# Who makes which half of an attention tile: GpSimd on first halves only, VectorE on both

## The chip, the core and the metric

The kernel runs on one core of a Trainium2 chip. The core has a matrix engine (TensorE, PE in the profile), a vector engine (VectorE, DVE), an activation engine (ScalarE, ACT), a general engine (GpSimd, POOL) and a queue engine for transfers (SyncE, SP). Each takes its instructions in its own order and waits for others through semaphores. The metric is the time of one execution on the device, in microseconds.

## What is computed

The input is `x` of 64 x 256 x 128 (64 graphs, 256 nodes, 128 features) and one 256 x 256 adjacency matrix. Four layers follow one another; each starts with a layer norm and a relu, and adds its result to `x`. Layer 0 is a gated unit of five steps, layer 1 a Chebyshev convolution, layer 2 a graph convolution with a norm. The last one matters here:

```python
s1 = jnp.einsum('bkf,ef->bke', x, W1)
s2 = jnp.einsum('bkf,ef->bke', x, W2)
pre = s1[:, :, None, :] + s2[:, None, :, :] + b_lin
h = jnp.where(pre >= 0, pre, ALPHA * pre)
e = jnp.einsum('bije,e->bij', h, a) + bias
attn = jax.nn.softmax(e, axis=2)
out = jax.nn.sigmoid(jnp.einsum('bij,bjf->bif', attn, x))
```

Here `W`, the weight matrix of the layer, is the adjacency matrix itself, so `e` runs over 256 features. For each of the 64 graphs, `pre` has 256 x 256 x 256 elements: a nonlinear function of every pair of nodes and every feature, which must be made element by element and then summed over the features with weights `a`.

## The kernel before

**Pairs and slots.** Graphs are taken two at a time: 32 pairs (`NPAIR`). The weights are folded in beforehand, and features are sorted by the sign of their weight, so that what is left of the nonlinear part is a maximum of s1 and -s2 (up to terms that are added elsewhere), times +1 or -1. The 256 features are two halves of 128, one feature to a partition. The first half is called a, the second b. For each pair there are 64 slots (`SLOTS`); a slot stands for a set of rows i of the attention matrix, and each of its two halves is one tile of 128 x 2048 elements: four groups of rows, two graphs, 256 nodes. In all there are 2048 slots (`NSLOT`), so 4096 half tiles. Seventeen tile buffers (`rl`, `TILES`) are shared by all of them.

**Who can make a half.** Each engine has its own form (`work_on_tile`, line 969):

- VectorE makes a whole tile in one instruction, a minimum of the broadcast `s1` and of the product `s2`, which it reads from the PSUM bank that TensorE wrote (line 988).
- ScalarE makes it in eight instructions, relu of `s1 - s2`, with `s1` as the bias and `s2` from its PSUM bank (line 996).
- GpSimd makes it in eight instructions, a minimum with a scalar, from copies of `s2` in SBUF, since it doesn't read PSUM here (line 1002). The copies are made by ScalarE: `s2c` for the first half (line 769) and `s2n` for the second (line 808).

`part_of` (line 925) says which kind an engine takes next. There are three kinds: 0 is a first half, 1 is a second half that is scored by itself, 2 is a second half that is summed onto its first half before both are scored as one tile. Before the change VectorE always takes kind 0, ScalarE always kind 1, and GpSimd takes kind 2 whenever that is not more than two slots ahead of the others (`AHEAD_OF`), and otherwise whichever of 0 and 1 lags.

**Summed slots.** For one third of the slots (`JOINED`, 650 of them, none among the last 96) the two halves are added by a DMA that accumulates, mostly two slots to a transfer (`add_pair`, line 1036). GpSimd issues it. TensorE then scores the sum once and not the halves twice.

**Scoring.** `score` (line 1090) multiplies a tile with a window of weights into a PSUM bank that collects the scores of 32 rows x 4 groups; `win` is for tiles of ScalarE and `win_n` for the others, with the opposite sign. Then `tail` makes the softmax and the output.

**The front.** `front` (line 512) computes layers 0 to 2 of a pair and the operands of layer 3, while the slots of the pair before are worked on. Its end touches the change: product `s2a` into a bank (765), copy `s2c` (769), product `s2b` into another bank (804), copy `s2n` (808), `s1b` (816) and `s1a` (825). The banks stay taken until the last half that reads them is made: `left` counts these, and `work_on_tile` gives a bank back to `spare` (line 1012).

**What sets the order.** The program is written out by a planner in the kernel's own Python (from line 1165). It keeps a clock for each engine, with an assumed duration for every kind of step (2.2 us for a VectorE tile, 1.46 us for four relus of ScalarE, 0.873 us for two instructions of GpSimd), takes the engine whose clock is least, and lets it do what is ready: steps of a tail first, then of a front (held back so that it doesn't run ahead), then half tiles; for TensorE scores come last. `in_order` ties the instructions of each engine to this order. The framework below adds semaphore waits between engines for every dependence that it sees, on tiles and on PSUM banks; the planner doesn't see these waits, only its own readiness times.

Of the kernel before, what the change touches and what calls it, by code (L numbers as in the profile page):

```python
# [10 lines left out]
OP = mybir.AluOpType  # L11
# [11 lines left out]
PE, DVE, ACT, POOL = ENGINES = (mybir.EngineType.PE, mybir.EngineType.DVE, mybir.EngineType.Activation, mybir.EngineType.Pool)  # L23
SLOTS = 64
SHARE = (1, 3)
AHEAD_OF = 2
ALONE = 96
LOW = 1
TILES = 17
# [4 lines left out]
def kernel(  # L34
# [50 lines left out]
    nc = tc.nc  # L85
    B, N, D = x.shape
# [34 lines left out]
    def ran(engine, us, *after):  # L121
        start = max(clock[engine], 0.0, *after)
        clock[engine] = start + us
        return clock[engine] + SEEN[engine]
# [6 lines left out]
    spare = [[b, 0.0] for b in banks]  # L131
# [26 lines left out]
    last, done = {}, [0]  # L158
# [325 lines left out]
    PROJECT, MIX, TURN, PRODUCT, PRODUCTS = (None, 0.44, 0.86), (None, 0.88, 1.74), (None, 0.48, 0.70), (None, 0.45, 0.88), (None, 1.33, 2.64)  # L484
    COPY, BIASED, TANH, ELEMENTS = (None, 0.34, 0.50), (None, 0.40, 0.59), (None, 0.41, 0.59), (None, 0.36, 0.61)
# [23 lines left out]
    READY = {}  # L509
    OF_FIRST = {}  # L510

    def front(p, batches):
# [4 lines left out]
        nb = len(batches)  # L517
# [18 lines left out]
        def kept(name, shape, **kw):  # L536

            if not alone:
                return work.tile([P, NB, *shape], F32, name=name, **kw)
            if name not in OF_FIRST:  # L540
                OF_FIRST[name] = work.tile([P, NB, *shape], F32, name=name, **kw)
            return OF_FIRST[name][:, own]

        def seen(b):
            return by_feature(b[0], nb)
# [14 lines left out]
        t = yield from norm(x0, 20.0 if p else 3.0, h)  # L560
        yield PE, t, 1
        b = take()
        to_feature(b[0], h)
        t_h = t
        t = ran(PE, TURN[nb], t, b[1])
        yield ACT, t
        hT, t_hT = copied("hT", b, t)
        for step in range(STEPS):
            yield PE, t_h, 1, lambda: "adj" in SET_UP
            b = take()  # L570
            mix_nodes(b[0], h, adj_t)
            t = ran(PE, MIX[nb], t_h, b[1])
            yield ACT, t
            mT, t_m = copied("h", b, t)
            if alone:
# [6 lines left out]
                t = ran(PE, PROJECT[nb], t_m)  # L582
# [5 lines left out]
                r = take()  # L588
            else:
# [4 lines left out]
                t = ran(PE, 2 * PROJECT[nb], t_m, t_hT, pr[1])  # L594
                yield ACT, t, 1
                r = take()
            nc.scalar.activation(seen(r), seen(pr), AF.Tanh, bias=br, scale=0.5)  # L597
            t = ran(ACT, TANH[nb], t, r[1])
# [5 lines left out]
            if alone:  # L604
# [5 lines left out]
                t = ran(PE, PROJECT[nb], t_rh)  # L610
            else:
# [6 lines left out]
                t = ran(PE, 2 * PROJECT[nb], t_rh, pv[1])  # L618
# [6 lines left out]
            if alone:  # L625
                nc.scalar.activation(seen(pv), seen(pv), AF.Tanh, bias=bh, scale=1.0)
                t = ran(ACT, TANH[nb], t)
                yield DVE, t
                nc.vector.tensor_sub(d, seen(pv), hT)
                t = ran(DVE, ELEMENTS[nb], t)  # L630
                spare.append([pv[0], t])
            else:
                nc.scalar.activation(seen(pv), seen(pv), AF.Tanh, bias=bh_n, scale=-1.0)  # L633
                t = ran(ACT, TANH[nb], t)
                yield DVE, t
                nc.vector.tensor_add(d, seen(pv), hT)  # L636
                t = ran(DVE, ELEMENTS[nb], t)
# [3 lines left out]
            t = ran(DVE, ELEMENTS[nb], t, t_z)  # L641
# [4 lines left out]
            t_hT = ran(DVE, ELEMENTS[nb])  # L646
            spare.append([pr[0], t_hT])
            yield PE, t_hT, 1
            b = take()
            to_token(b[0], hT)  # L650
            t = ran(PE, TURN[nb], t_hT, b[1])
# [9 lines left out]
        t = ran(DVE, ELEMENTS[nb], t)  # L661
# [6 lines left out]
        b = take()  # L668
        mix_nodes(b[0], h, adj_n)
        t = ran(PE, MIX[nb], t_h, b[1])  # L670
# [3 lines left out]
        b = take()  # L674
        to_feature(b[0], h)
        t = ran(PE, TURN[nb], t_h, b[1])
        yield ACT, t
        hT, t = copied("hT", b, t)
# [6 lines left out]
        b = take()  # L685
        mix_nodes(b[0], h, adj_2)
        t = ran(PE, MIX[nb], t_h, b[1])
        yield ACT, t
        c2T, t = copied("h", b, t)
# [5 lines left out]
        t = ran(PE, PRODUCTS[nb], t, t_po)  # L695
        yield DVE, t
        if alone:
            pt = rows_of(turned_of(po))
            nc.vector.tensor_add(pt, pt, bias1.unsqueeze(1).to_broadcast([P, nb * NC, D]))
            t = ran(DVE, ELEMENTS[nb], t)  # L700
# [3 lines left out]
        t = ran(DVE, ELEMENTS[nb])  # L704
# [4 lines left out]
        t = yield from norm(x2, t, h)  # L709
# [7 lines left out]
        b = take()  # L717
        mix_nodes(b[0], h, adj_ti)
        t = ran(PE, MIX[nb], t, b[1])
        yield ACT, t  # L720
        yT, t = copied("h", b, t)
# [5 lines left out]
        t = ran(PE, PRODUCT[nb], t, t_po)  # L727
        if alone:
# [3 lines left out]
            t = ran(DVE, ELEMENTS[nb], t)  # L732
# [3 lines left out]
        t = ran(ACT, COPY[nb], t)  # L736
# [3 lines left out]
        t = ran(DVE, ELEMENTS[nb], t)  # L740
        yield POOL, t
        inverse_root(rn, rn, MOST_POSITIVE, OP.min, NORM_EPS * NORM_EPS, OP.max)
        t = ran(POOL, 1.45, t)

        yield DVE, t, 0, lambda: p < 2 or (p - 2, NC - 1) in TAILED
        x3 = kept("x3", [NC, D])
# [3 lines left out]
        t = ran(DVE, LAST[nb], t)  # L750
# [3 lines left out]
        h3 = kept("h3", [NC, D + 1])  # L754
        nc.gpsimd.memset(h3[:, :, :, D:D + 1], 2.0)
        t = yield from norm(x3, t, h3)
        yield PE, t, 1
        b = take()
        to_feature(b[0], h3)
        t = ran(PE, TURN[nb], t, b[1])  # L760
        yield ACT, t
        hT, t_hT = copied("hT", b, t)
        yield PE, t_hT, 1
        s2a = take()
# [3 lines left out]
        s2c = kept("s2c", [N])  # L768
# [3 lines left out]
        b = take()  # L772
# [4 lines left out]
        t = ran(PE, 0.25, t_hT, b[1])  # L777
# [4 lines left out]
        t = ran(ACT, 0.2, t)  # L782
# [6 lines left out]
        s1o = kept("s1o", [NC])  # L789
# [3 lines left out]
        for k in range(2):  # L793
            nc.sync.dma_start(row[k, 0:nb * N].rearrange("(q g i) -> g q i", g=4, i=32),
                              quarter[k:P:32, 0:cols].rearrange("g (q i) -> g q i", i=32))
            t = moved(t) if k else max(t, moved(t) - 2.2)
        rows = kept("rows", [2, N])[:, 0] if alone else work.tile([P, 2, NB, N], F32, name="rows")
        nc.sync.dma_start(rows if alone else rows.rearrange("p k b n -> p k (b n)"), row[:, 0:nb * N].unsqueeze(0).to_broadcast([P, 2, nb * N]))
        lin, s2o = (rows[:, k].unsqueeze(1) if alone else rows[:, k] for k in range(2))
        t = moved(t) + 1.5  # L800
        t_lin = t
        yield PE, t_hT, 1
        s2b = take()
        project(s2b[0], w2n[:, P:2 * P], hT)
        t = ran(PE, PROJECT[nb], t_hT, s2b[1])
        yield ACT, t
        s2n = kept("s2n", [N])
        nc.scalar.copy(s2n, seen(s2b))
        t_2 = ran(ACT, COPY[nb], t)
        yield PE, t_hT, 1  # L810
        b = take()
        project(b[0], w1[:, P:2 * P], hT)
        t = ran(PE, PROJECT[nb], t_hT, b[1])
        yield ACT, t
        s1b = kept("s1b", [N])
# [4 lines left out]
        b = take()  # L820
        project(b[0], w1[:, 0:P], hT)
        t = ran(PE, PROJECT[nb], t_hT, b[1])
        yield ACT, t
        s1a = kept("s1a", [N])
        nc.scalar.activation(s1a, seen(b), AF.Identity, bias=blin_s[:, 0:1], scale=1.0)
        t_n = ran(ACT, BIASED[nb], t)
        spare.append([b[0], t_n])
        ops = dict(x3=x3, h3=h3, s1=(s1a, s1b), s2a=seen(s2a), s2b=seen(s2b), bank=[s2a, s2b], s2c=s2c, s2n=s2n, s1o=s1o, s2o=s2o,
                   lin=lin, t_lin=t_lin, since=(max(t_n, t_s2a), max(t_b, t_2), max(t_b, t_2)), alone=alone,
                   left=[0, 0])  # L830
        for u in batches:
            READY[p, u] = ops
            for n in range(p * SLOTS + u * SLOTS // 2, p * SLOTS + (u + 1) * SLOTS // 2):
                ops["left"][0] += 1
                ops["left"][1] += n not in WITH
        tiles.extend([t, max(t_b, t_n, t_lin)] for t, _ in lent)

    def across(u):
# [66 lines left out]
    begun = {}  # L905
    made = []
    left = {}
# [3 lines left out]
    WITH = set(JOINED)  # L911
# [6 lines left out]
    def where(n):  # L918
        return (n // SLOTS, n % SLOTS // 32), n % 32

    def slot(k):

        return ORDER[k][following[k]] if following[k] < len(ORDER[k]) else NSLOT

    def part_of(e):

        if e == DVE:
            return 0
        if e == ACT:
            return 1  # L930
        if slot(2) <= max(slot(0), slot(1)) + AHEAD_OF:
            return 2
        return 0 if slot(0) < slot(1) else 1

    def tile_ready(e):

# [9 lines left out]
    def row_of(u, s1, r):  # L946

        i = s1.rearrange("p b (c g i) -> p g c b i", c=NC, g=4)
        return i[:, :, :, 0, r:r + 1] if READY[u]["alone"] else i[:, :, u[1], :, r:r + 1]
# [19 lines left out]
    def work_on_tile(e):  # L969
        if e not in begun:  # L970
            k = part_of(e)
            begun[e] = [slot(k), k, *chosen(slot(k), k), 0]
            following[k] += 1
            held[e] += 1
            if k < 2:
                READY[where(begun[e][0])[0]]["left"][k] -= 1
        n, k, t, free, part = begun[e]
        u, r = where(n)
        ops = READY[u]
        rows = row_of(u, ops["s1"][min(k, 1)], r)  # L980
        since = max(ops["since"][k], free)

        def other(s2, b):
            return s2[:, 0 if ops["alone"] else b, :]

        if e == DVE:
            whole = [P, 4, NB, N]
            nc.vector.tensor_tensor(t, rows.to_broadcast(whole), ops["s2a"].unsqueeze(1).to_broadcast(whole), op=OP.min)  # L988
            done = ran(DVE, 2.2, since)
            ops["bank"][0][1] = max(ops["bank"][0][1], done)  # L990
            parts = 1
        elif e == ACT:
            parts = 2
            for g in (2 * part, 2 * part + 1):
                for b in range(NB):
                    nc.scalar.activation(t[:, g, b, :], other(ops["s2b"], b), AF.Relu, bias=rows[:, g, b], scale=-1.0)  # L996
            done = ran(ACT, 1.46, since)
            ops["bank"][1][1] = max(ops["bank"][1][1], done)
        else:
            parts = 4  # L1000
            for b in range(NB):
                nc.gpsimd.tensor_scalar(t[:, part, b, :], other(ops["s2n" if k else "s2c"], b), rows[:, part, b],  # L1002
                                        MOST_NEGATIVE, op0=OP.min, op1=OP.max)
            done = ran(POOL, 0.873, since)
        begun[e][4] += 1
        if part + 1 == parts:
            del begun[e]
            if n in WITH:
                pairs.setdefault(n, {})[k] = done, t, e
            else:  # L1010
                made.append((done, n, k, t, e))
        if k < 2 and not ops["left"][k] and ops["bank"][k] and not any(b[1] == k and where(b[0])[0] == u for b in begun.values()):
            spare.append(ops["bank"][k])
            ops["bank"][k] = None

    def pair_ready():

# [220 lines left out]
```

## Time and profile before

| what | value |
|---|---|
| median of 3 runs | 4700.0 us (4699.17 to 4700.02) |
| the profiled execution | 4698.46 us |
| its span, first to last instruction | 4696.7 us |
| granted TensorE clock, mean | 0.999 |
| DMA queue of the additions (POOL's) | 80.2% of 16 engines |

The page gives for each engine its busy time, its share of the span and its number of instructions; a chain of waits, which is followed back from the last instruction; and groups of instructions by line and shape, with busy time, mean duration and the idle time of the engine just before them. Instructions of one engine overlap each other, so the mean duration of one is longer than the time that one more of them adds (busy time divided by number, or the pitch in a timeline).

In steady state all four engines work through: between 2000 and 3000 us PE is busy 997.13 us, DVE 993.53, ACT 990.51 and POOL 988.76.

### The profile page before, as it was taken

How to read it: one execution, taken by the hardware profiler on the slowest of the kernel's cores; microseconds unless marked ns; L12 is line 12 of the kernel's file. 1: busy time of each engine (PE TensorE's matmuls, PEld its weight loads, DVE VectorE, ACT ScalarE, POOL GpSimd, SP SyncE). 2: the span in 40 equal slices, each digit the busy share in tenths (PEclk: the TensorE clock that was granted, in tenths of full speed). 3: DMA queues.
4: the chain of work that ended last, by engine and by line, in shares of the span. 5: the costliest groups of instructions: out<-in, count | busy, mean ns of one | idle time of the engine just before them, and what ended most of it. 6: DMA issues, size and time to landing. Idle time of an engine off the chain costs nothing.

```text
span 4696.7 us, 131312 instructions
## 1 busy us (share of the span) xinstructions
PE 4665.0 (99%) x51191; PEld 1765.1 (38%) x51191; DVE 4602.0 (98%) x3646; ACT 4590.1 (98%) x11987; POOL 4540.5 (97%) x9757
## 2 busy tenths in 40 slices
PE   9999999999999999999999999999999999999999
PEld 4433333433333433433333343333333333333333
DVE  5999999999999999999999999999999999999998
ACT  5999999999999999999999999999999999999999
POOL 2999999999999999999999999999999999999998
PEclk9999999999999999999999999999999999999999
DMA  1888998889988898988988989889888898898840
GB/s 28 168 159 164 167 168 161 162 159 168 167 164 165 155 167 162 170 167 156 166 166 162 168 161 168 163 166 168 160 160 167 163 169 165 161 162 165 159 78 4
DMA packets 133930, 725.02 MB, mean 154 GB/s; under 512 B 10936, under 2 KB 46136, under 8 KB 50104
## 3 DMA queue, kind: packets, MB, share of 16 engines
q0 software_dynamic: 88800, 681.60, 80.2%
q1 hardware_dynamic: 43784, 35.01, 2.5%
q8 instruction: 400, 6.55, 0.5%
q14 instruction: 226, 1.85, 0.1%
q10 hardware_dynamic: 720, 0.00, 0.0%
HBM read 26.48 MB, written 8.52 MB: 7 GB/s over the span
## 4 chain that ended last, share of the span: by engine, by line
PE 83%; DVE 7%; ACT 4%; POOL 4%; DMA 1%; issue 1%; POOLq 0%; DVEq 0%; ACTq 0%
PE bank L1106 53%; PE bank L428 26%; DVE rl L988 6%; POOL rl L1002 3%; ACT rl L996 3%; PE bank L461 2%; DMA rl<-rl 1%; PE bank L453 1%; ACT h L506 0%; POOL mv L423 0%; POOL rl L1053 0%; DVE r L636 0%; DVE bank L640 0%; DVE hT L644 0%; PE bank L776 0%
## 5 line engine op out<-in xcount | busy, mean ns | idle before, releaser
L988 DVE TENSOR_TENSOR rl<-s1a,bank 128x2048 f32<-128x2048 f32 x1757 | 3925.4, 2275 | 7.1 <-PE bank L1106 3.6
L996 ACT ACTIVATE rl<-bank,s1b 128x256 f32<-128x256 f32 x9808 | 3886.1, 710 | 0.9 <-PE bank L1106 0.3
L1002 POOL TENSOR_SCALAR rl<-s2n,s1b 128x256 f32<-128x256 f32 x6576 | 3054.4, 698 | 18.7 <-ACT s1b L816 7.5
L1106 PE MATMUL bank<-rl,win_n 128*32 128x512 f32 x17760 | 2250.5, 593 | 8.0 <-DVE rl L988 4.6
L1106 PE MATMUL bank<-rl,win 128*32 128x512 f32 x9808 | 1321.4, 593 | 0.0
L1002 POOL TENSOR_SCALAR rl<-s2c,s1a 128x256 f32<-128x256 f32 x2328 | 1083.2, 616 | 3.1
L1106 PEld LDWEIGHTS bank<-rl,win_n 128*32 128x32 f32 x17760 | 601.3, 110 | 1156.4 <-issue 959.7
L1106 PEld LDWEIGHTS bank<-rl,win 128*32 128x32 f32 x9808 | 336.6, 110 | 630.2 <-issue 508.8
L428 PE MATMUL bank<-h,wts 128*32 128x512 f32 x3720 | 467.1, 592 | 0.8 <-ACT bank L597 0.8
L1053 POOL DMA_DIRECT2D rl<-rl x350 | 406.9, 1174 | 4.3 <-POOL rl L1002 3.3
L428 PE MATMUL bank<-adj_t,h 128*32 128x256 f32 x4960 | 302.0, 381 | 2.3 <-ACT h L655 1.9
L428 PEld LDWEIGHTS bank<-h,wts 128*32 128x32 f32 x3720 | 126.1, 110 | 265.3 <-issue 209.1
L428 PEld LDWEIGHTS bank<-adj_t,h 128*32 128x32 f32 x4960 | 164.1, 110 | 160.6 <-issue 48.5
L553 ACT COPY h<-bank 128x512 f32<-128x512 f32 x217 | 166.3, 780 | 16.2 <-PE bank L428 14.9
L506 ACT ACTIVATE h<-xin,mv 128x128 f32<-128x128 f32 x372 | 166.2, 631 | 16.0 <-POOL mv L502 15.4
L428 PE MATMUL bank<-hT,wts 128*32 128x512 f32 x1240 | 167.0, 593 | 0.0
L428 PE MATMUL bank<-r,u5t 128*32 128x512 f32 x1240 | 166.8, 592 | 0.0
L597 ACT ACTIVATE bank<-bank,gate_b 128x512 f32<-128x512 f32 (+1 forms) x165 | 136.0, 824 | 17.1 <-PE bank L428 12.8
L423 POOL TENSOR_TENSOR mv<-mv,minus_half 128x4 f32<-128x4 f32 (+1 forms) x132 | 133.7, 1013 | 11.0
L620 ACT ACTIVATE bank<-bank,gate_b 128x512 f32<-128x512 f32 (+1 forms) x165 | 133.7, 810 | 9.3 <-PE bank L428 9.1
L633 ACT ACTIVATE bank<-bank,gate_b 128x512 f32<-128x512 f32 x155 | 129.0, 832 | 2.9 <-PE bank L428 2.9
L636 DVE TENSOR_TENSOR r<-bank,hT 128x512 f32<-128x512 f32 x155 | 105.6, 681 | 14.9 <-ACT bank L633 14.6
(204 smaller groups left out, 2983.0 us busy)
## 6 DMA issues: line engine op xcount, KB each, us to landing
rl<-rl POOLq DMA_DIRECT2D x300, 2048.0 KB, 14.7
rl<-rl POOLq DMA_DIRECT2D x50, 1024.0 KB, 12.1
rows<-row SPq DMA_DIRECT2D x31, 512.0 KB
xin<-in_x_dram SPq DMA_DIRECT2D x64, 128.0 KB
out_dram<-o SPq DMA_DIRECT2D x63, 128.0 KB
row<-r SPq DMA_DIRECT2D x62, 2.0 KB
rows<-row SPq DMA_DIRECT2D x2, 256.0 KB
rl<-in_L_gnn_w_w_dram SPq DMA_DIRECT2D x3, 128.0 KB
```

Source lines behind the costliest of these rows:

```text
L423: nc.gpsimd.tensor_tensor(t, t, minus_half[:, 0:t.shape[1]], op=OP.pow)
L428: nc.tensor.matmul(o[g:g + 32], w[:, g:g + 32], t, start=start, stop=stop, skip_group_check=True)
L506: nc.scalar.activation(h[:, k, :], s[:, k, :], AF.Relu, bias=mv[:, k, 0:1], scale=mv[:, k, 1:2])
L553: nc.scalar.copy(c, seen(bank))
L597: nc.scalar.activation(seen(r), seen(pr), AF.Tanh, bias=br, scale=0.5)
L620: nc.scalar.activation(seen(pr), seen(pr), AF.Tanh, bias=bz, scale=0.5)
L633: nc.scalar.activation(seen(pv), seen(pv), AF.Tanh, bias=bh_n, scale=-1.0)
L988: nc.vector.tensor_tensor(t, rows.to_broadcast(whole), ops["s2a"].unsqueeze(1).to_broadcast(whole), op=OP.min)
L996: nc.scalar.activation(t[:, g, b, :], other(ops["s2b"], b), AF.Relu, bias=rows[:, g, b], scale=-1.0)
L1002: nc.gpsimd.tensor_scalar(t[:, part, b, :], other(ops["s2n" if k else "s2c"], b), rows[:, part, b], MOST_NEGATIVE, op0=OP.min, op1=OP.max)
L1053: nc.gpsimd.dma_start(out=into, in_=of, accum_op=OP.add, max_dma_last_dim=8192)
L1106: nc.tensor.matmul(pe[g * 32:(g + 1) * 32, :], w[:, 31 - r:63 - r], flat(t[:, g]), start=False, stop=(left[u] == 0), skip_group_check=True)
```

## The change

GpSimd makes first halves only. VectorE makes every second half that is summed (kind 2) and otherwise first or second halves, whichever lags; ScalarE goes on making second halves that are scored alone. VectorE reads the second operand where ScalarE reads it, in the PSUM bank of `s2b`. So the copy `s2n` is dropped, and the count that gives back the bank of `s2b` now includes the summed second halves.

```diff
+LEAD = 0
...
         s2b = take()
         project(s2b[0], w2n[:, P:2 * P], hT)
-        t = ran(PE, PROJECT[nb], t_hT, s2b[1])
-        yield ACT, t
-        s2n = kept("s2n", [N])
-        nc.scalar.copy(s2n, seen(s2b))
-        t_2 = ran(ACT, COPY[nb], t)
+        t_2 = ran(PE, PROJECT[nb], t_hT, s2b[1])
...
-                ops["left"][1] += n not in WITH
+                ops["left"][1] += 1
...
     def part_of(e):
 
-        if e == DVE:
+        if e == POOL:
             return 0
         if e == ACT:
             return 1
         if slot(2) <= max(slot(0), slot(1)) + AHEAD_OF:
             return 2
-        return 0 if slot(0) < slot(1) else 1
+        return 0 if slot(0) <= slot(1) + LEAD else 1
...
-            if k < 2:
-                READY[where(begun[e][0])[0]]["left"][k] -= 1
+            READY[where(begun[e][0])[0]]["left"][min(k, 1)] -= 1
...
-            nc.vector.tensor_tensor(t, rows.to_broadcast(whole), ops["s2a"].unsqueeze(1).to_broadcast(whole), op=OP.min)
+            nc.vector.tensor_tensor(t, rows.to_broadcast(whole), (ops["s2b"] if half else ops["s2a"]).unsqueeze(1).to_broadcast(whole), op=OP.min)
             done = ran(DVE, 2.2, since)
-            ops["bank"][0][1] = max(ops["bank"][0][1], done)
+            ops["bank"][half][1] = max(ops["bank"][half][1], done)
...
-                nc.gpsimd.tensor_scalar(t[:, part, b, :], other(ops["s2n" if k else "s2c"], b), rows[:, part, b],
+                nc.gpsimd.tensor_scalar(t[:, part, b, :], other(ops["s2c"], b), rows[:, part, b],
                                         MOST_NEGATIVE, op0=OP.min, op1=OP.max)
...
-        if k < 2 and not ops["left"][k] and ops["bank"][k] and not any(b[1] == k and where(b[0])[0] == u for b in begun.values()):
-            spare.append(ops["bank"][k])
-            ops["bank"][k] = None
+        if not ops["left"][half] and ops["bank"][half] and not any(min(b[1], 1) == half and where(b[0])[0] == u for b in begun.values()):
+            spare.append(ops["bank"][half])
+            ops["bank"][half] = None
```

Every line after 27 has another number in the changed kernel: the tile instructions are at 985 (VectorE), 993 (ScalarE) and 999 (GpSimd) there, the scores at 1103.

## The prediction

> **What bounds the kernel now.** I read the page's first part, then its chain of waits.
>
> ```profile
> span 4696.7 us, 131312 instructions
> PE 4665.0 (99%) x51191; PEld 1765.1 (38%) x51191; DVE 4602.0 (98%) x3646; ACT 4590.1 (98%) x11987; POOL 4540.5 (97%) x9757
> ```
>
> ```profile
> PE 83%; DVE 7%; ACT 4%; POOL 4%; DMA 1%; issue 1%; POOLq 0%; DVEq 0%; ACTq 0%
> ```
>
> All four compute engines are full; TensorE ends the chain by a nose (83% of it). An edit that only moves work between DVE, ACT and POOL can therefore gain little: PE's own 4665.0 us remain. But every engine has only 30 to 155 us of idle time, so a new wait on any of them shows in the span at once. Next the costliest groups, which are the halves that the change redistributes.
>
> ```profile
> L988 DVE TENSOR_TENSOR rl<-s1a,bank 128x2048 f32<-128x2048 f32 x1757 | 3925.4, 2275 | 7.1 <-PE bank L1106 3.6
> L996 ACT ACTIVATE rl<-bank,s1b 128x256 f32<-128x256 f32 x9808 | 3886.1, 710 | 0.9 <-PE bank L1106 0.3
> L1002 POOL TENSOR_SCALAR rl<-s2n,s1b 128x256 f32<-128x256 f32 x6576 | 3054.4, 698 | 18.7 <-ACT s1b L816 7.5
> ...
> L1002 POOL TENSOR_SCALAR rl<-s2c,s1a 128x256 f32<-128x256 f32 x2328 | 1083.2, 616 | 3.1
> ```
>
> The names after the arrow matter. DVE reads s1a and a PSUM bank (the product s2a); ACT reads s1b and another PSUM bank (s2b); POOL reads only copies in SBUF, of which s2n is the one that goes away. So today the bank of s2b has one steady reader, ACT, and the bank of s2a has one, DVE. The idle column says that neither ever waits for the other: 0.9 us before ACT's 9808 instructions, 7.1 us before DVE's 1757.
>
> **The change by parts.** The copy that goes is this group (all instructions of ACT by form):
>
> ```profile
> L808 ACT COPY s2n<-bank 128x512 f32<-128x512 f32 x31 | 22.4, 721 | 0.2
> ...
> L808 ACT COPY s2n<-bank 128x256 f32<-128x256 f32 x2 | 0.8, 379 | 0.0
> ```
>
> 33 copies, 23.2 us counted with overlap. ACT's instructions overlap each other, so I price by pitch, from the timeline near the end, where both engines run one kind alone:
>
> ```profile
> 4658.45 24.26 DVE L988 TENSOR_TENSOR rl<-s1a,bank 128x2048 f32<-128x2048 f32 x11
> 4659.25 28.24 ACT L996 ACTIVATE rl<-bank,s1b 128x256 f32<-128x256 f32 x76
> ```
>
> (Start, duration, what.) A DVE tile takes (24.26 - 2.275) / 10 = 2.20 us. An ACT relu takes (28.24 - 0.67) / 75 = 0.368 us, 0.67 being its median duration. ACT's other 2179 instructions then take (4590.1 - 9808 x 0.368) / 2179 = 0.45 us each. The copies are thus worth 33 x 0.45 = 15 us of ACT. That is the whole gain that the change offers, and as PE is the bound, little of it could reach the end.
>
> POOL's halves cost the same from either operand: 3054.4 / 6576 = 0.464 us and 1083.2 / 2328 = 0.465 us. In the built program the amounts hardly move: DVE 1751 tiles (932 first halves, 819 second) for 1757, ACT 9832 relus for 9808, POOL 8928 instructions for 8904, 347 additions by DMA (303 double, 44 single) for 350; PE's instructions are the same in number. So: DVE -6 x 2.2 = -13 us, ACT +24 x 0.368 = +9, POOL +24 x 0.464 = +11; all lie beside PE's work. GpSimd's queue holds 3 issues fewer (1.17 us each), and SP's transfers are the same.
>
> **What it adds.** DVE's 819 second halves read the same PSUM bank that ACT's relus read. The waits in the built program say what becomes of that: 770 of the 819 DVE tiles carry a wait for the last ACT relu on that bank, and 793 ACT relus carry a wait for a DVE second-half tile on that bank. In the program of before no relu waits for a DVE tile that reads its bank (122 wait for a DVE first half, for other reasons). Both engines run their queues in order, so the bank is used in turns: ACT finishes its group, DVE makes its tile while ACT's next relu stands in the queue, then ACT goes on. The kernel's planner knows nothing of this: it wrote the order as if both ran at once.
>
> By operand, the order has 773 places where DVE's second-half tiles (783 of them; 10 places have two) stand between two ACT groups of one pair; the other 36 stand at a pair's ends, where ACT is already or still on another bank, and block nothing. I call the 773 places stops and sum ACT's time line over the span:
>
> - ACT's work: 4590.1 - 15 + 9 = 4584 us.
> - DVE's tiles in the stops, ACT standing still: 783 x 2.20 = 1723 us.
> - The hand-over, twice per stop. The nearest rows (timelines of the start and of the end):
>
> ```profile
> 45.03 0.45 ACT L597 ACTIVATE bank<-bank,gate_b 128x256 f32<-128x256 f32 x1 [1.75 <-PE bank L428]
> 45.51 0.42 DVE L601 SCALAR_TENSOR_TENSOR rl<-bank,rl 128x256 f32<-128x256 f32 x1 [0.74 <-ACT bank L597]
> ...
> 4690.02 0.08 DVE L856 DVE_READ_ACCUMULATOR2_ANT nmx<- 128x1 f32 x1
> ...
> 4690.14 0.91 ACT L863 ACTIVATE sc<-sc,nmx 128x256 f32<-128x256 f32 x2 [2.66 <-DVE nmx L856]
> ```
>
>   45.51 - 45.48 = 0.03 us from ACT to DVE, 4690.14 - 4690.10 = 0.04 back. Besides, an engine that must drain pays its last instruction in full and not by pitch: DVE 2.275 - 2.20 = 0.075, ACT at least 0.45 (the shortest relu) - 0.368 = 0.08, at most 0.710 (the mean) - 0.368 = 0.34. That makes 0.23 to 0.49 us per stop. I take 0.25, near the lower end, since a group that starts after a pause runs as the short rows do: 773 x 0.25 = 193 us.
> - What hides: ACT's instructions that read other things and stand in its queue within a stop. 758 stops have a wait on both sides; 314 of these have none in between, 245 one, 97 two, the rest more. At 0.45 us each and at most a stop's length, that is 396 us.
> - Stops at which DVE comes later than ACT. Between two stops ACT has 5.5 us of work on the average (4153 / 758) and DVE 3.9 (2919 / 758); pricing each gap by both, DVE is the later in 54, by 57 us together.
> - ACT's idle time of before stays: 4696.7 - 4590.1 = 107 us, of which 51 lie in the first 150 us.
> - New waits for PE, POOL and the additions, since the planned order no longer fits: no row shows them. Bounds: nothing, and three times the 107 us, 321. I take 56, the idle time outside the start once more, as PE, POOL and DMA all get slack.
>
> Sum: 4584 + 1723 + 193 - 396 + 57 + 107 + 56 = 6324 us of span. The profiled execution has 1.8 us around its span (4698.46 - 4696.7), and the median of the runs shown is 1.5 above it: 6324 + 3 = 6327, say 6330 us, or +35%.
>
> Behind ACT's blocked relu stand the front's copies and tanh (PE waits for them), behind DVE's blocked tile its gate products; each of these moves with the two engines. PE needs 4665 us of 6330, POOL about 4550: neither takes over. DMA's 80% on the additions' queue thins to 60%.
>
> The Trainium skill speaks against the change, in PSUM — Partial Sum Buffer, section "PSUM bank collisions raise a hardware error": two engines on one bank and partition quadrant at once are an error, reads against reads included, so software has to keep them apart. No row of before shows two such readers. By that rule the waits can't be spared, and the sum is the one above; were such reads free, it would be 4690.
>
> PE will now pause often, so its clock counts. The granted clock was 0.95 from 80 to 100 us, where PE was busy 16.75 of 20 us, and 0.68 in the last 7 us, where it was busy 2.0. It would decide only if it fell below 4665 / 6330 = 0.74 on the average. TensorE: Matmul & The Clock Gate, "Part 1: The HAM clock gate", says that the clock halves after an idle window of about 3.4 us. At half clock throughout PE's work would be 9330 us by that page; pauses as long as a stop (2.5 us) are shorter than its window.
>
> **Rivals.**
> 1. The bank alone. All of ACT's other work slips into the stops or into gaps: 9832 x 0.368 + 1723 + 193 + 57 + 107 = 5698 us. For it: ACT's other work (980 us) is shorter than the stops. Against it: ACT's queue is in order, and 314 of 758 stops have nothing to slip in. Anything up to 6100 I count here: 0.09.
> 2. Turn-taking spreads. A DVE tile that waits for its buffer, which PE frees late, holds ACT as well. Price: another 0.7 us per stop, 773 x 0.7 = 541, so 6870 us. For it: 606 of the 819 DVE tiles also wait for PE. Against: PE idles a quarter of the time. 0.11.
> 3. No slower: the stops fall where ACT pauses anyway, and the 15 us of copies decide. Price: 4700 - 15 = 4685 at best. It decides only if a stop costs ACT under 15 / 773 = 0.02 us, against 2.20 + 0.25 = 2.45 as worked out, and ACT has 107 us of pauses to hide 1723. 0.01; that the change doesn't do what it says is excluded by the built program, where the copies are gone and the tiles are moved. 0.01 for that the bound is elsewhere in an unseen way and time stays equal.
>
> The forecast has 0.78. A measurement of this kernel tells 0.2% (9 us) from no change: faster 0.01, same 0.01, slower 0.98.
>
> **The range.** Downwards, hand-over at 0.23 (-15), no DVE lateness (-57), relus at the pitch of eight in mid-kernel, 2.84 / 8 = 0.355 (9832 x 0.013 = -128): 6130, and some of rival 1: 6090. Upwards, hand-over at 0.49 (+185) and waits at half their bound (+105) give 6620, and part of rival 2: 6700.
>
> **What would show it.** ACT's idle time before L993 (L996 of before) grows from 0.9 us to well over 1200 us, nearly all released by DVE's L985; DVE's before L985 grows too, released by ACT's L993. Busy shares fall to about 73% on all four engines, the chain alternates DVE and ACT, PE's share of it collapses. DVE's tile stays at 2275 ns, with s1b as with s1a. I am wrong if ACT's idle time is named after PE or DMA, if the granted clock is under 0.9, or if DVE and ACT records on one bank overlap.

## The result, and the profile after

The changed kernel takes 6191.44 us (median of 6 runs, 6189.27 to 6193.57) against 4700.1 us before: a ratio of 1.3172, with a 95% interval of 1.3155 to 1.3189. It was forecast at 6330 us. The first lines of its page:

```profile
span 6190.9 us, 131780 instructions
PE 5305.7 (86%) x51191; PEld 1870.1 (30%) x51191; DVE 4660.6 (75%) x3640; ACT 4652.3 (75%) x11978; POOL 4589.2 (74%) x9778
```

The work is the same: ACT, DVE and POOL are busy for 49 to 62 us more than before, in a span that is 1494 us longer. All three stand still a quarter of the time. The groups say where (the last columns are the idle time of the engine just before the group, and what ended most of it):

```profile
L993 ACT ACTIVATE rl<-bank,s1b 128x256 f32<-128x256 f32 x9832 | 3792.6, 533 | 1459.6 <-DVE rl L985 1350.2
L999 POOL TENSOR_SCALAR rl<-s2c,s1a 128x256 f32<-128x256 f32 x8928 | 4060.4, 588 | 387.3 <-PE bank L1103 335.8
L985 DVE TENSOR_TENSOR rl<-s1b,bank 128x2048 f32<-128x2048 f32 x819 | 1871.8, 2287 | 1367.2 <-ACT rl L993 1319.6
...
L985 DVE TENSOR_TENSOR rl<-s1a,bank 128x2048 f32<-128x2048 f32 x932 | 2102.8, 2279 | 0.7 <-PE bank L1103 0.4
```

ACT's relus waited 0.9 us in all before the change and wait 1459.6 now. DVE's first halves, whose bank nobody else reads all the time, wait 0.7 us; its second halves wait 1367.2, ended by ACT's relus. Neither engine's instruction got longer: the DVE tile takes 2279 ns with s1a and 2287 with s1b. The list of who waited for whom gives the numbers of waits (sum in us, times, longest):

```profile
ACT rl L993 <- DVE rl L985: 1350.2, 692, 3.6
DVE rl L985 <- ACT rl L993: 1319.6, 699, 4.8
```

The other 109 us of the 1459.6 are named after PE, POOL and the like, but they are turns too: of the 752 pauses of ACT before a relu, 751 end within 0.2 us after a second half of DVE on the same bank (the records of the trace, put beside the operands in the built program).

And the timeline of ACT and DVE shows two such turns (start, duration; in brackets the idle time before):

```profile
3011.75 1.59 ACT L993 ACTIVATE rl<-bank,s1b 128x256 f32<-128x256 f32 x4
3013.37 2.29 DVE L985 TENSOR_TENSOR rl<-s1b,bank 128x2048 f32<-128x2048 f32 x1 [3.02 <-ACT rl L993]
3015.69 1.57 ACT L993 ACTIVATE rl<-bank,s1b 128x256 f32<-128x256 f32 x4 [2.35 <-DVE rl L985]
```

ACT ends four relus at 3013.34, DVE starts 0.03 us later, ends at 3015.66, ACT starts 0.03 us later, and so on. Nowhere in this stretch do the two run together on the bank, and in the whole trace no record of the 819 second halves overlaps a relu on the same bank. DVE waited 3.02 us for its turn, and ACT then 2.35 us for its own.

The chain of waits no longer helps: it is followed back over 15% of the span only, and there it alternates between ACT (7%) and DVE (4%).

### The profile page after: what moved, and what is told of

The parts are those of the page before. It is cut to its first block, busy times and chain, and to the rows that moved or that the text cites. A ratio compares the mean times of both kernels' runs of the same rounds, so it can differ in the third digit from the quotient of the medians.

```text
span 6190.9 us, 131780 instructions
## 1 busy us (share of the span) xinstructions
PE 5305.7 (86%) x51191; PEld 1870.1 (30%) x51191; DVE 4660.6 (75%) x3640; ACT 4652.3 (75%) x11978; POOL 4589.2 (74%) x9778
## 5 line engine op out<-in xcount | busy, mean ns | idle before, releaser
L993 ACT ACTIVATE rl<-bank,s1b 128x256 f32<-128x256 f32 x9832 | 3792.6, 533 | 1459.6 <-DVE rl L985 1350.2
L999 POOL TENSOR_SCALAR rl<-s2c,s1a 128x256 f32<-128x256 f32 x8928 | 4060.4, 588 | 387.3 <-PE bank L1103 335.8
L985 DVE TENSOR_TENSOR rl<-s1b,bank 128x2048 f32<-128x2048 f32 x819 | 1871.8, 2287 | 1367.2 <-ACT rl L993 1319.6
L1103 PE MATMUL bank<-rl,win_n 128*32 128x512 f32 x17736 | 2388.4, 608 | 47.3 <-DVE rl L985 46.6
L985 DVE TENSOR_TENSOR rl<-s1a,bank 128x2048 f32<-128x2048 f32 x932 | 2102.8, 2279 | 0.7 <-PE bank L1103 0.4
L1103 PE MATMUL bank<-rl,win 128*32 128x512 f32 x9832 | 1711.1, 613 | 84.4 <-ACT rl L993 83.6
L1103 PEld LDWEIGHTS bank<-rl,win 128*32 128x32 f32 x9832 | 403.4, 112 | 1021.6 <-issue 503.6
L462 PE MATMUL bank<-ident,hT 128*128 128x128 f32 x620 | 108.1, 300 | 124.7 <-DVE hT L645 104.0
L462 PEld LDWEIGHTS bank<-ident,hT 128*128 128x128 f32 x620 | 69.5, 147 | 245.8 <-DVE hT L645 148.2
L602 DVE SCALAR_TENSOR_TENSOR r<-bank,hT 128x512 f32<-128x512 f32 x155 | 106.5, 687 | 34.4 <-ACT bank L598 34.2
```

Source lines behind the costliest of these rows:

```text
L462: nc.tensor.transpose(pt[:, b, c, :], ht[:, b, c * P:(c + 1) * P], ident)
L602: nc.vector.scalar_tensor_tensor(rh, seen(r), 1.0, hT, op0=OP.add, op1=OP.mult)
L985: nc.vector.tensor_tensor(t, rows.to_broadcast(whole), (ops["s2b"] if half else ops["s2a"]).unsqueeze(1).to_broadcast(whole), op=OP.min)
L999: nc.gpsimd.tensor_scalar(t[:, part, b, :], other(ops["s2c"], b), rows[:, part, b], MOST_NEGATIVE, op0=OP.min, op1=OP.max)
L1103: nc.tensor.matmul(pe[g * 32:(g + 1) * 32, :], w[:, 31 - r:63 - r], flat(t[:, g]), start=False, stop=(left[u] == 0), skip_group_check=True)
```

## The experiments

The theory is that turns on one PSUM bank cost the time. Its rivals are that VectorE's second halves are late or slow for another reason, and that the planner's order of work is upset by who makes what. Ratios are to the kernel before on the same chip (there 4710 to 4720 us).

**VectorE reads an SBUF copy.** The copy `s2n` comes back, and VectorE's second halves read it; ScalarE has the bank alone.

```diff
+        s2n = kept("s2n", [N])
+        nc.scalar.copy(s2n, seen(s2b))
...
-(ops["s2b"] if half else ops["s2a"]).unsqueeze(1)
+(ops["s2n"] if half else ops["s2a"]).unsqueeze(1)
```

> VectorE's second halves read an SBUF copy of s2b (made by ScalarE, as before the change), ScalarE's relus the bank alone; who makes which half is as in the changed kernel. Theory (turns on one PSUM bank cost the time): the idle time of ScalarE before its relus falls from 1460 us to under 50 and the time to 4700-4740 us. Rival (moving second halves to VectorE and the new order of work cost the time, whatever they read): 6000 us or more.

Measured: 6386.71 us, ratio 1.3531 (1.3511 to 1.3551). By the time alone the theory had fallen. The page of this run says otherwise:

```profile
PE 5500.2 (86%) x51191; PEld 1882.9 (30%) x51191; DVE 5392.9 (85%) x3644; ACT 4639.4 (73%) x11979; POOL 6172.7 (97%) x9780
...
L1003 POOL TENSOR_SCALAR rl<-s2c,s1a 128x256 f32<-128x256 f32 x8928 | 5593.2, 777 | 26.9 <-PE bank L1107 8.5
L997 ACT ACTIVATE rl<-bank,s1b 128x256 f32<-128x256 f32 x9800 | 3779.8, 574 | 120.9 <-PE bank L1107 80.6
...
L989 DVE TENSOR_TENSOR rl<-s1b,s2n 128x2048 f32<-128x2048 f32 x823 | 2633.0, 3213 | 108.3 <-PE bank L1107 80.3
L989 DVE TENSOR_TENSOR rl<-s1a,bank 128x2048 f32<-128x2048 f32 x932 | 2104.0, 2276 | 138.6 <-PE bank L1107 136.9
```

ACT and DVE hardly wait for each other any more (DVE 6.6 us for ACT, ACT not at all by name); but GpSimd's work has grown from 4060.4 to 5593.2 us for the same 8928 instructions, and VectorE's tile takes 3213 ns on the average when both its operands lie in SBUF, 2276 when one lies in PSUM. GpSimd is now the full engine, at 97%. The timeline of the two:

```profile
3000.01 10.93 POOL L1003 TENSOR_SCALAR rl<-s2c,s1a 128x256 f32<-128x256 f32 x24
...
3005.38 7.94 DVE L989 TENSOR_TENSOR rl<-s1b,s2n 128x2048 f32<-128x2048 f32 x1
...
3011.60 28.46 POOL L1003 TENSOR_SCALAR rl<-s2c,s1a 128x256 f32<-128x256 f32 x32
...
3025.83 4.76 DVE L989 TENSOR_TENSOR rl<-s1b,s2n 128x2048 f32<-128x2048 f32 x2
```

First GpSimd runs through at 10.93 / 24 = 0.46 us each, and VectorE's one tile beside it takes 7.94 us. Then VectorE's tiles from SBUF take their usual 2.3 to 2.5 us, two of them 4.76, and GpSimd's 32 instructions beside them 28.46 us, or 0.89 each. One of the two holds the other up, now this one and now that. So one new obstacle had taken the place of the old one, and this run could not decide between the theories by its time.

**ScalarE reads the SBUF copy.** The same copy, given to the other engine; VectorE has the bank alone.

```diff
-nc.scalar.activation(t[:, g, b, :], other(ops["s2b"], b), AF.Relu, bias=rows[:, g, b], scale=-1.0)
+nc.scalar.activation(t[:, g, b, :], other(ops["s2n"], b), AF.Relu, bias=rows[:, g, b], scale=-1.0)
```

> The other way round: ScalarE's relus read the SBUF copy, VectorE has the bank of s2b alone. Theory: again no turns, 4700-4800 us if a relu from SBUF costs ScalarE the 0.37 us that it costs from the bank; each 0.01 us more per relu is 98 us of ScalarE. Rival (VectorE's tiles are slow or late for another reason): 6000 us or more.

Measured: 4966.91 us, ratio 1.052 (1.0503 to 1.0538). Who makes what is nearly as in the changed kernel (823 second halves of VectorE for 819), and of its 31.7% of loss 5.2% are left.

```profile
PE 4806.3 (97%) x51191; PEld 1796.6 (36%) x51191; DVE 4619.5 (93%) x3644; ACT 4905.7 (99%) x11979; POOL 4585.5 (92%) x9780
...
L997 ACT ACTIVATE rl<-s2n,s1b 128x256 f32<-128x256 f32 x9800 | 4065.7, 529 | 0.0
...
L989 DVE TENSOR_TENSOR rl<-s1b,bank 128x2048 f32<-128x2048 f32 x823 | 1862.1, 2277 | 8.0 <-PE bank L1107 7.7
```

ACT's relus wait 0.0 us and DVE's second halves 8.0. What remains over the kernel before is ACT itself, at 99%: with 0.45 us for each of its 2179 other instructions a relu from SBUF takes (4905.7 - 981) / 9800 = 0.40 us, 0.03 more than from the bank.

**The same, with the planner told of it.** `ran(ACT, 1.46, since)` becomes `ran(ACT, 1.60, since)` in the kernel of the run above.

> ScalarE's relus read the SBUF copy as in e2, and the planner is told 1.60 us instead of 1.46 for four of them, so that it gives ScalarE fewer tiles. ScalarE's 98% bound eases: its 0.027 us more per relu x 9800 = 265 us, shared among three engines at 0.98 tiles per us, is about 85 us of time: 4760-4830 us (4967 in e2). If a relu from SBUF were not what e2 was bound by: 4930 or more.

Measured: 4828.31 us, ratio 1.0229 (1.0214 to 1.0245). ScalarE got 9200 relus and all four engines are at 97 to 99%. So the run above was bound by its ScalarE, and nothing else shows behind it.

**A second bank, filled by TensorE.** No copy in SBUF; the product is made twice, and each engine reads its own.

```diff
+        s2d = take()
+        project(s2d[0], w2n[:, P:2 * P], hT)
...
-(ops["s2b"] if half else ops["s2a"]).unsqueeze(1)
+(ops["s2d"] if half else ops["s2a"]).unsqueeze(1)
```

> TensorE makes the product s2b twice, into two PSUM banks: ScalarE's relus read the one, VectorE's second halves the other, and there is no SBUF copy of it. Theory (turns on one bank in the changed kernel, a shared SBUF read path of VectorE and GpSimd in the run with the copy): both disappear, no idle time between VectorE and ScalarE, VectorE's tile 2.28 us with either operand, GpSimd's pitch 0.465 us; TensorE gets 32 more products of 0.86 us = 28 us, so 4700-4760 us. Rival (second halves on VectorE upset the order of work): 5000 us or more.

Measured: 4771.42 us, ratio 1.01 (1.0087 to 1.0114), 11 us above what was expected (the kernel before took 4719 us on that chip, where the expectation counts from 4700). The groups that shared a bank before:

```profile
L997 ACT ACTIVATE rl<-bank,s1b 128x256 f32<-128x256 f32 x9880 | 3864.3, 688 | 36.1 <-PE bank L1109 20.0
...
L989 DVE TENSOR_TENSOR rl<-s1b,bank 128x2048 f32<-128x2048 f32 x813 | 1839.4, 2276 | 37.6 <-PE bank L1109 14.6
```

This is the whole change, with neither a shared bank nor a second operand in SBUF, and the loss of 31.7% shrinks to 1.0%. Moving the halves costs about 1%; sharing the bank was the cost.

**A second bank, filled by ScalarE's copy.**

```diff
+        s2d = take()
+        nc.scalar.copy(seen(s2d), seen(s2b))
```

> As the run before, but the second bank is filled by ScalarE's copy from the first, so TensorE's work is that of the kernel before and ScalarE copies two operands again. Theory: 4690-4740 us, TensorE the bound; against the run before it shows what a product more on TensorE costs (28 us if TensorE is the bound, 0 to 10 if it isn't).

Measured: 4762.48 us, ratio 1.0082 (1.0067 to 1.0096), 22 us above what was expected. Against the run with TensorE's second product it is 9 us less, where 28 had been possible, with overlapping intervals. The 0.8% that stay go with small waits for PE and for the additions (ACT's relus 39 us, VectorE's two groups 52, GpSimd's 44, where the kernel before has 0.9, 7.1 and 21.8). A third bank held by each pair may cause them; that wasn't tried.

**Half the dose.** In the odd pairs VectorE reads the second bank, in the even ones the shared one.

```diff
-(ops["s2d"] if half else ops["s2a"]).unsqueeze(1)
+((ops["s2d"] if u[0] % 2 else ops["s2b"]) if half else ops["s2a"]).unsqueeze(1)
```

> The dose again, without the SBUF operand: in the odd pairs VectorE reads the second bank (as in the run with the bank copy, 4762 us), in the even pairs the bank of ScalarE (as in the changed kernel, 6191 us). 393 relus wait for a VectorE tile on their bank, for 793. Theory: half way, (4762 + 6191) / 2 = 5477 us (5380-5580), ScalarE's idle time before its relus near 730 us. Rival (one disturbance upsets the whole order): above 5700.

Measured: 5476.98 us, ratio 1.1625 (1.1592 to 1.1659); idle time before ACT's relus 755.9 us. The cost is in proportion to the number of turns: over the run with the bank copy it is 0.154 of the time before for the 359 waits of ACT named after DVE, and 0.309 for 692 in the changed kernel. Three stretches of this run (PE, PEld, DVE, ACT, POOL busy, clock, DMA), below the line of its waits, show that it comes and goes with the pairs, which take 5477 / 32 = 171 us each:

```profile
ACT rl L999 <- DVE rl L990: 695.0, 359, 3.7
...
1000.00:1100.00 100.00, 100.00 (x1141) 37.27 (x1136) 97.82 (x80) 94.87 (x249) 96.39 (x209) 1.00 0.84 156
...
1200.00:1300.00 100.00, 82.08 (x791) 27.23 (x787) 77.02 (x59) 76.05 (x199) 78.53 (x168) 0.97 0.61 121
1300.00:1400.00 100.00, 99.74 (x1109) 39.03 (x1105) 96.55 (x79) 97.36 (x254) 91.47 (x198) 1.00 0.81 149
```

**Half the dose with the SBUF copy.** The same idea, tried earlier, with `s2n` in place of the second bank.

> In the odd pairs VectorE reads the SBUF copy, in the even pairs the shared bank as in the changed kernel. Theory: the cost goes with the number of stops, so half of 1491 us remains: 4700 + 745 = 5445 us (5300-5600), in alternating stretches, full in odd pairs and about 75% busy in even ones. Rival (the order slips once and stays late): nearer 6190 than 5445, and no alternation.

Measured: 6170.9 us, ratio 1.3071 (1.3045 to 1.3097). A miss, since it rested on the SBUF copy being free. It has both obstacles in one run:

```profile
L989 DVE TENSOR_TENSOR rl<-s1b,s2n 128x2048 f32<-128x2048 f32 x409 | 1294.7, 3180 | 28.8 <-PE bank L1107 12.8
L989 DVE TENSOR_TENSOR rl<-s1b,bank 128x2048 f32<-128x2048 f32 x414 | 945.8, 2287 | 691.5 <-ACT rl L997 669.0
```

The tiles from SBUF are long (3180 ns) and hardly wait; those from the shared bank are short (2287 ns) and wait 691.5 us.

**The SBUF operand by itself.** In the kernel before, VectorE's first halves read `s2c`; nothing else is changed.

```diff
-rows.to_broadcast(whole), ops["s2a"].unsqueeze(1).to_broadcast(whole)
+rows.to_broadcast(whole), ops["s2c"].unsqueeze(1).to_broadcast(whole)
```

> The kernel before the change, but VectorE's first halves read the SBUF copy s2c (which is there for GpSimd) and not the bank of s2a: nothing is moved between engines. It measures the disputed cost of e1 by itself. Theory (VectorE with two SBUF operands and GpSimd's reads exclude each other): VectorE's 1757 tiles x 2.20 = 3865 us and GpSimd's 8904 x 0.456 = 4060 us follow one another, with GpSimd's other 470 us behind: 7900-8800 us. Rival (the slowness of e1 comes from the moved second halves): 4700-4750.

Measured: 8257.39 us, ratio 1.7527 (1.7476 to 1.7578).

```profile
L1002 POOL TENSOR_SCALAR rl<-s2n,s1b 128x256 f32<-128x256 f32 x6576 | 5773.8, 1062 | 17.7 <-ACT s1b L816 7.5
L988 DVE TENSOR_TENSOR rl<-s1a,s2c 128x2048 f32<-128x2048 f32 x1757 | 4872.3, 2809 | 990.8 <-PE bank L1106 775.3
```

GpSimd's 6576 instructions take 5773.8 us for 3054.4 before. The price of the first run is thus no matter of the change.

**The planner is told of the turns.** In the changed kernel each pair keeps when VectorE and ScalarE last leave the bank; the other starts after that.

```diff
+        turn = READY[where(n)[0]]["turn"]
+        wait = turn[DVE] if e == ACT else turn[ACT] if e == DVE and k else 0.0
+        return max(since[k], min(t[1] for t in tiles), wait)
...
+            if half:
+                ops["turn"][DVE] = clock[DVE] + 0.1
...
+            ops["turn"][ACT] = clock[ACT] + 0.1
```

> The changed kernel, with the turns on the bank told to the planner: it keeps for each pair when VectorE's last second half and ScalarE's last relus on the bank end, and starts the other engine after that. In the built order ScalarE has 8792 relus (9832), VectorE 949 second and 643 first halves, GpSimd 1405 first halves; 908 second halves stand in 542 stops. Theory: turns can be arranged better but not spared: ScalarE 8792 x 0.368 + 973 = 4208, + 908 x 2.2 = 1998, + 542 x 0.25 = 135, + 80 idle, less 400-600 hidden: 5820-6020 us. Rival (the loss is the planner's ignorance, waits that a right order avoids): 4700-5000 us.

Measured: 5738.62 us, ratio 1.2155 (1.2131 to 1.2179). Better than the changed kernel's 1.3172, and 81 us under the expected range. Its engines, and ACT's waits for DVE:

```profile
PE 5375.8 (94%) x51191; PEld 1928.8 (34%) x51191; DVE 4301.0 (75%) x3481; ACT 4266.0 (74%) x10938; POOL 5584.9 (97%) x12073
...
ACT rl L1001 <- DVE rl L991: 1018.8, 470, 10.4
```

The turns are fewer (470 waits of ACT for 692) and the total is smaller, but they stay. The expected sum was wrong in two terms: ACT's relus waited 1044.5 us where the 908 tiles and the hand-overs come to 1998 + 135, so about 1090 us were hidden and not 400 to 600; and ACT's other idle time was 5736.9 - 4266.0 - 1044.5 = 426 us and not 80. This run doesn't show how well turns can be arranged, since the planner moved work as well: GpSimd makes 1405 first halves for 1116 and is the full engine now, at 97%, so that this order could not have taken much less than its 5584.9 us.

**What the copy is worth.** The kernel before with `nc.scalar.copy(s2n, seen(s2b))` made twice.

> The kernel before with the copy s2n made twice (32 x 0.45 = 15 us more on ScalarE). It measures what the copy that the change takes away is worth. Theory: at most its own 15 us: 4700 + 0 to 12. Rival (a copy on ScalarE delays the operands and with them every engine, so that taking it away could have gained much): more than 25 us.

Measured: a ratio of 1.0009 (1.0001 to 1.0018), which is 4 us (0 to 8) for 33 copies more on ScalarE. The planner was told of them and gave ScalarE 9768 relus for 9808, so a part of their 15 us was made up elsewhere. That is the size of the gain the change could have had.

## Why the prediction was right

**The bound and the gain.** That PE and all the others were full, and that 33 copies could give 15 us at best, held: making the copy twice costs 4 us.

**The amounts.** DVE's 932 and 819 tiles, ACT's 9832 relus and POOL's 8928 instructions are in the page as counted in the built program.

**The turns.** The mechanism was the one forecast: ACT's wait is named after DVE's second halves, and DVE's after ACT's relus. The two runs with a second bank and the run with half the shared pairs show it as the cause. The rival that stops fall into ACT's pauses had a turning point of 0.02 us per stop; a wait of ACT that is named after DVE took 1350.2 / 692 = 1.95 us on the average. The turns are semaphore waits of the program, which the framework sets; the runs show their price, and not what the chip would do without them.

**The sum**, in three parts of ACT's time line:

| part | forecast, us | measured, us |
|---|---|---|
| ACT busy, with 0.08 us per stop for draining | 4584 + 62 = 4646 | 4652 |
| ACT idle in the stops | 1723 + 131 - 396 + 57 = 1515 | 1460 |
| other idle time of ACT | 107 + 56 = 163 | 6191 - 4652 - 1460 = 79 |
| span | 6324 | 6191 |

The hand-over was taken at 0.25 us. The two turns shown above give it: 2.35 us from ACT's end to its start, plus 0.085 for draining (four relus take 1.57 us and more of them 0.371 each), less 2.20, is 0.235. The most mis-sized step is the last of the list: the allowance of 56 us for new waits on PE, POOL and the additions, and with it the idle time of before that was to stay. There was no allowance to make: all but one of ACT's pauses before relus are turns, and its other idle time fell from 107 to 79 us. Presumably PE and POOL, with 14% and 26% of their time free, were early where they had been just in time. Another 55 us are in the stops. The records, put beside the operands in the built program, give all 773 of them. ACT's other work hides 439 us there (forecast 396), and DVE is late in 68 stops by 37 us together (forecast 54 stops and 57 us). 315 stops have nothing of ACT's in between (forecast 314), and ACT stands still in 749.

**Rivals.** The bank alone (5698 us) was out of reach in the planner's order: 439 us of ACT's 980 slipped into the stops. That the run with the planner told came to 5738.62 us, close to this rival's price, is chance: it has other amounts and another full engine. Waits that spread further (6870 us) did not come.

**The two pages of the Trainium skill.** What PSUM — Partial Sum Buffer says of two engines on one bank ("PSUM bank collisions raise a hardware error") agrees with the waits in the built program; no run here let the two collide, so the error itself isn't shown. The granted clock fell to 0.956 on the average, far above the 0.74 from which it would have decided. But comparing a stop of 2.5 us with a window of 3.4 us was too mild: the trace has 134 stretches at half clock, of 3.4 us and up to 6.8, 549 us together, and only 45 pauses of PE longer than 3.4 us, so shorter pauses were enough at times. PE's busy share was forecast at about 73% and is 86%, 5305.7 us for 4665.0. The clock would make 4665.0 / 0.956 = 4880 us of it, and the scoring matmuls are recorded with 608 to 613 ns for 593; where the rest comes from no run shows.

**What it lacked.** The operand's place was looked at for the bank alone. That a copy in SBUF would have been no remedy for VectorE wasn't seen until the first experiment's expectation was missed by 1650 us.

## What to carry to other kernels

Before an engine is given work because it has the time, look at where its operands lie and who else reads there: in this program two engines that read one PSUM bank run in turns, kept apart by semaphores, and the price is the whole duration of the one, each time, for the other. The waits that the built program carries show it before any run; count how many times the two alternate, multiply by the tile, and subtract only what stands in the queue between. The remedy for the turns was a bank for each reader (1.008 to 1.010 of the time before). A copy in SBUF cost 2.3% with ScalarE as its reader and the planner told, and 35% with VectorE. No form of the change was faster than the kernel before.

## What the runs showed of the hardware that wasn't expected

VectorE with two operands in SBUF and GpSimd hold each other up. By its median it looks mild: VectorE's tile has 2408 ns in the run with `s2c` (2276 before), but its longest takes 16353, and the larger group of GpSimd's instructions takes 1062 ns on the average for 698. As an estimate of full exclusion, VectorE's 1757 x 2.20 us and GpSimd's 4540.5 us of before add up to 8406 us; measured were 8257.39. The Trainium skill has the rule in SBUF — State Buffer, section "Who interferes with whom": a VectorE instruction with two SBUF inputs contends with a GpSimd instruction that reads SBUF. The tiles with one operand in PSUM, at 2275 to 2287 ns in every run, agree with it.

ScalarE's relu takes 0.40 us with its input in SBUF and 0.37 us with it in a PSUM bank. On the full engine this 0.03 us made 5.2% of the time, and 2.3% with the planner told of it.
